# Selective scan on one core: VectorE's products half a group earlier, and ScalarE adding the carried state to 30 of 32 scans

## The chip, the core and the metric

The kernel runs on one core of one Trainium2 chip. A core has TensorE (PE, with its weight loads PEld), VectorE (DVE), ScalarE (ACT), GpSimd (POOL) and SyncE (SP, which only issues DMAs here). Each engine takes its instructions in the order in which the program lists them and waits on semaphores for the others. The metric is the device time of the whole program in microseconds.

## The reference, cut to what matters

The program is a chain of four layers on an image of shape (2, 128, 64, 64). The first three (attention, a deformable convolution block, a residual convolution block) are not touched. The fourth normalises every pixel over its channels, runs a selective scan ("mamba") over the 4096 pixels in four orders (by rows, by columns, and both reversed), and fuses the four results:

```python
def _mamba(x, W_in, conv_w, conv_b, W_xp, W_dt, b_dt, A_log, Dp, W_out):
    ...
    dt = jax.nn.softplus(dt @ W_dt.T + b_dt)
    A = -jnp.exp(A_log)
    dA = jnp.exp(dt[..., None] * A)                        # 256 channels x 16 states
    dBu = dt[..., None] * Bm[:, :, None, :] * xh[..., None]
    def step(h, inp):
        dA_t, dBu_t = inp
        h = dA_t * h + dBu_t
        return (h, h)
    ...
    y = jnp.einsum('lbdn,bln->bld', hs, Cm)
    y = y + xh * Dp
    y = y * jax.nn.silu(z)
    return y @ W_out.T
```

So for each of 256 x 16 = 4096 pairs of channel and state a first-order recurrence runs along 4096 pixels, for two images and four orders.

## The kernel before, in words

**Blocks, groups, scans.** `layer3` cuts each of the 2 x 4 sequences into 8 blocks of 512 pixels (`BLK`): 64 blocks, numbered `i`. A block has 8 groups, one for each half of the channels (`hf`) and each quarter of the states (`ng`); `k` numbers the 512 groups and `slot = k % 8` is a group's place in its block. A group has 4 scans `q` of 128 partitions x 512 pixels, so a block has 32 scans. In this document "scan 2.1" is scan `q = 1` of the group at slot 2.

**What one group needs.** PE copies the row of B to 128 partitions into a bank of PSUM (`pb`, L1692). The product B x (dt x u) for all four scans goes into an SBUF tile `db`: the first `ND[hf][ng]` columns by DVE (`db_dve`, L1713), the rest by POOL (`db_pool`, L1722). Before, DVE does five whole groups of a block and 176 of the 512 columns of slot 2; POOL does slots 1 and 6 whole and 336 columns of slot 2. ACT computes `da = exp(dt*A)` for each scan into one of three PSUM buffers (`expo`, L1735), two scans ahead of DVE (`AHEAD = 2`). DVE runs the recurrence in place (`scan`, L1749). ACT keeps the last column of the four scans (`keep`, L1754, into `hl`), POOL multiplies the group by C (`cmul`, L1759, in place, after `keep` has read it), and PE sums it over the states (`sums`, L1767).

**The carried state.** A scan of a block that isn't the first of its sequence starts from the state that the last block left. Either DVE reads it as the scan's initial value (operand `hl` in the profile's rows, "hl form" below), or ACT adds it to the first column of `db` ahead of time (L1741, 128x1) and the scan starts from zero; the kernel calls such a scan carried. Before, 20 of 32 scans are carried: all of slots 1 and 6, whose products POOL makes two groups ahead, and scans 2 and 3 of the others. L1741 directly follows the `expo` of its scan.

**The order.** Everything is issued in the order of one hand-written loop over `k` (`tc.manual_schedule`). Inside, a loop over `q` issues `expo` of the scan two ahead and then `scan(k, q)`. After the four scans come `db_dve(k + 1)`, `cmul(k - 1)`, `db_pool(k + 2)` and the work for the next block, a part for each slot. Its ACT part (`front_act`) is: slot 0 two copies of the x-projection; slot 1 a softplus of four activations (L1652 to L1655); slot 2 another, and a copy; slot 3 two copies; slot 4 a Silu of z between two table loads; slot 7 a Silu of u between two table loads. Its PE part (`front_pe`) makes what these read. `finish`, one ACT copy of 128x512, stands in slot 6 before the last `expo`. The DMAs of a group (`transfers`) stand ahead of its loop over `q`.

**Two kinds of blocks with more work.** In blocks 0 to 4 and 22 to 29 a further 512 pixels are normalised alongside ("LN blocks", 13 of 64; `next_norm`). The two matmuls of that, mean at slot 0 and variance at slot 2 (L1517, L1534), write to the same three PSUM buffers as `da`; the logarithm (`ln_log`, L1538) stands before `expo` in `q == 3` of slot 2, the store (`ln_store`, L1553) at the end of slot 6. In blocks 1 to 4 and 33 to 36 ("turn blocks") ACT also copies two pieces of the image into the other order at the end of slot 6 (`turn`, L1559).

Of the kernel before, what the change touches and what calls it, by code (L numbers as in the profile page):

```python
# [15 lines left out]
AF = mybir.ActivationFunctionType  # L16
# [8 lines left out]
BLK = 512  # L25
NBLK = L // BLK
# [1394 lines left out]
def layer3(g, I, out):  # L1421
# [5 lines left out]
    nc, tc = g.nc, g.tc  # L1427
    NJ = 4

    ND = ((BLK, 0, 176, BLK), (BLK, BLK, 0, BLK))  # L1430
    NNG = N_STATE // NJ
    HB = 1
    HC = 3
    with ExitStack() as ctx:
# [139 lines left out]
        NBK = len(blocks)  # L1574
# [134 lines left out]
        def db_dve(k):  # L1709
            i, hf, ng = groups[k]  # L1710
            n = ND[hf][ng]
            if n:
                nc.vector.tensor_tensor(  # L1713
                    db_tile(k)[:, :, :n], G[k].pop("pb")[:, :n].unsqueeze(1).to_broadcast([P, 4, n]),
                    S[i]["d4", hf][:, 1, :, :n], ALU.mult,
                )
# [9 lines left out]

        def carried(k, q):

            i, hf, ng = groups[k]
            return i % NBLK > 0 and (q >= 2 or ND[hf][ng] == 0)  # L1730

        def expo(k, q):
            i, hf, ng = groups[k]
            da = psd.tile([P, BLK], F32, name="da")
            nc.scalar.activation(da, S[i]["d4", hf][:, 0, q, :], AF.Exp, scale=am[:, hf, q, ng : ng + 1])  # L1735
            G[k]["da", q] = da
            if carried(k, q):

                first = BLK - 1 if reverse(i) else 0
                b0 = G[k]["db"][:, q, first : first + 1]  # L1740
                nc.scalar.activation(b0, da[:, first : first + 1], AF.Identity, bias=b0, scale=hl[:, hf, ng, q, :])  # L1741

        def scan(k, q):
            i, hf, ng = groups[k]
# [6 lines left out]
        def keep(k):  # L1751
            i, hf, ng = groups[k]
            last = 0 if reverse(i) else BLK - 1
            nc.scalar.copy(hl[:, hf, ng], G[k]["db"][:, :, last : last + 1])  # L1754
# [6 lines left out]
        def sums(k):  # L1761
            i, hf, ng = groups[k]
            if ng == 0:
                py = S[i]["y", hf] = psy.tile([P, BLK], F32, name="py")
                nc.tensor.matmul(py, ddp[:, hf, :], S[i]["u"][:, hf, :], start=True, stop=False)
            for q in range(4):
                nc.tensor.matmul(  # L1767
                    S[i]["y", hf][32 * q : 32 * q + 32, :], fold, G[k]["db"][:, q, :],
                    start=False, stop=(ng == NNG - 1),
                )  # L1770
            del G[k]

        def gate(i, hf):
            s_ = S[i]
            gt = s_["gt", hf] = ck.tile([P, BLK], F32, name="gt")
            nc.vector.tensor_tensor(gt, s_.pop(("y", hf)), s_["z"][:, hf, :], ALU.mult)  # L1776
# [11 lines left out]
        def finish(i):  # L1788
            b, nd, c = blocks[i]
            s_ = S.pop(i)  # L1790
            if nd == 0:
                nc.scalar.activation(s_["xv"], img(s_["pf"]), AF.Identity, bias=vec(g, "b_fuse"))  # L1792
            elif nd < 3:
                nc.scalar.copy(s_["xv"], img(s_["pf"]))
            else:
                res = ck.tile([P, BLK], F32, name="res", bufs=1)
                nc.scalar.copy(res, s_["pf"])
                nc.sync.dma_start(out[b, :, c * BLK : (c + 1) * BLK], res)

        groups = [(i, hf, ng) for i in range(NBK) for hf in range(2) for ng in range(NNG)]  # L1800
        G = {}
# [75 lines left out]
        with tc.manual_schedule():  # L1877
            tc.keep_in_program_order(nc.scalar.preload_act_table_set("natural_log_exp_and_others"))
            nc.scalar.activation(am, am, AF.Exp)
            nc.vector.tensor_scalar(am, am, -1.0, None, ALU.mult)  # L1880
            nc.vector.memset(xt[:, :HC], 0.0)
            nc.vector.memset(xt[:, HC + L :], 0.0)
            nc.vector.memset(xn[:, HB - 1, HW - HC :], 0.0)
            nc.vector.memset(xn[:, HB + HW, :HC], 0.0)
            units = [(k, q) for k in range(len(groups)) for q in range(4)]
            AHEAD = 2

            for k in range(NFIRST):
                ln_mean(0, k)
            for k in range(NFIRST):  # L1890
                ln_less(0, k)
            ln_square(0, 0)
            ln_var(0, 0)
            ln_square(0, 1)
            ln_log(0, 0)
            ln_root(0, 0)
            ln_scale(0, 0)
            ln_var(0, 1)
            ln_square(0, 2)
            ln_store(0, 0)  # L1900
            ln_var(0, 2)
            begin(0)
            conv(0, 1)
            for part in (ln_log, ln_root, ln_scale):
                for k in (1, 2):
                    part(0, k)
            conv_silu(0)
            front_pe(0, 0)
            ln_store(0, 1)
            front_act(0, 0)  # L1910
            bc_store(0)
            front_pe(0, 1)
            front_act(0, 1)
            ln_store(0, 2)
            sum_parts(0, 0)
            sum_copy(0, 0)
            spread(0, 0)
            spread_store(0, 0)
            spread_load(0, 0)
            softplus(0, 1)  # L1920
            front_pe(0, 3)
            front_act(0, 3)
            spread(0, 1)
            spread_store(0, 1)
            for ng in range(NNG):
                copies(0, "b", ng)
                copies(0, "c", ng)
            for k in range(2):
                weights(k)
            db_dve(0)  # L1930
            db_pool(0)
            front_pe(0, 4)
            front_act(0, 4)
            front_pe(0, 5)
            front_pe(0, 6)
            for u in range(AHEAD):
                expo(*units[u])
            front_act(0, 7)
            db_pool(1)
            for k in range(len(groups) + 7):  # L1940
                i, slot = divmod(k, 8)
                live = k < len(groups)
                more = k + 1 < len(groups)
                ended = 1 <= k <= len(groups)
                transfers(i + 1, slot)
                if k + 2 < len(groups):
                    weights(k + 2)
                norm = next_norm(i)
                for q in range(4):
                    if slot == 6 and q == 3 and 1 <= i <= NBK:  # L1950
                        finish(i - 1)
                    if norm and slot == 2 and q == 3:
                        ln_log(*norm)
                    if q == 0 and ended:
                        keep(k - 1)
                    if 4 * k + q + AHEAD < len(units):
                        expo(*units[4 * k + q + AHEAD])
                    if norm and q == 0:
                        if slot == 0:
                            ln_mean(*norm)  # L1960
                        elif slot == 2:
                            ln_var(*norm)
                    if live:
                        scan(k, q)

                    for j, hf in (((k - 6) // 8, 0), ((k - 10) // 8, 1)):
                        if q == 1 and 8 * j + 6 + 4 * hf == k and 0 <= j < NBK:
                            gate(j, hf)
                if norm and slot == 0:
                    ln_less(*norm)  # L1970
                if more:
                    db_dve(k + 1)
                if ended:
                    cmul(k - 1)
                if k + 2 < len(groups):
                    db_pool(k + 2)

                if slot == 5 and 0 <= k - 2 < len(groups):
                    sums(k - 2)
                if slot == 5 and 1 <= i <= NBK:  # L1980
                    project(i - 1)
                front_pe(i + 1, slot)
                front_act(i + 1, slot)
                front_pool(i + 1, slot)
                if norm:
                    if slot == 1:
                        ln_square(*norm)
                    elif slot == 3:
                        ln_root(*norm)
                    elif slot == 5:  # L1990
                        ln_scale(*norm)
                    elif slot == 6:
                        ln_store(*norm)
                if live:

                    if slot == 6 and 0 < i % (4 * NBLK) <= NBLK // 2:
                        for n in range(2):
                            turn(blocks[i][0], 2 * (i % (4 * NBLK) - 1) + n)

                if slot != 5 and 0 <= k - 2 < len(groups):  # L2000
                    sums(k - 2)
# [155 lines left out]
```

## Time and profile before

| | us |
|---|---|
| median of 3 runs | 5483.52 (5479.7 to 5484.56) |
| the profiled execution | 5481.25 |
| its span in the profile | 5479.5 |

| engine | busy, share of the span | busy in 4000 to 4500 us of the span |
|---|---|---|
| PE | 4690.7 us, 86% | 403.89 of 500 us |
| DVE | 4537.5 us, 83% | 490.28 |
| ACT | 4062.2 us, 74% | 426.38 |
| POOL | 3646.3 us, 67% | 494.15 |

The first three layers end at about 2190 us; the scan of the 64 blocks takes the other 3.3 ms. Shares over the whole span mix the layers, so the last column, a stretch inside the scan, is the one to read. An instruction's record on DVE can overlap the next one's by some tens of ns, so the distance from start to start is what an instruction costs a full queue, not the length of its record.

### The profile page before, as it was taken

Reading aid. Unit: us, or ns where it says so; the run is one execution under the profiler, and the core shown is the slowest. Engines: PE = TensorE matmul, PEld = TensorE weight load, DVE = VectorE, ACT = ScalarE, POOL = GpSimd, SP = SyncE. Lnnn points to the kernel's source line nnn. Section 1 sums busy time; section 2 is a strip of 40 time slices with the busy share of each in tenths; the row PEclk is TensorE's granted clock in tenths of the full one; section 3 lists DMA queues with packets and bytes.
Section 4 is the critical chain, followed back from the end, with each engine's and each line's share of the span. In section 5 each row is a group of like instructions: output and inputs, shape, how many; then the busy total and the mean of one; then the engine's idle time right before and its main releaser. Section 6 shows DMA issues by size and latency. Waiting matters only on the chain.

```text
span 5479.5 us, 54616 instructions
## 1 busy us (share of the span) xinstructions
PE 4690.7 (86%) x17062; PEld 1753.3 (32%) x17062; DVE 4537.5 (83%) x4280; ACT 4062.2 (74%) x6242; POOL 3646.3 (67%) x1205
## 2 busy tenths in 40 slices
PE   7999999999996998778777887878888777888776
PEld 3444444344453443222222222222222222222221
DVE  7666655661356995999999999999999999999998
ACT  4999999500365114898888888888898888888886
POOL 5232222200001111999999999999999999999998
PEclk9999999999998999888888788888778888788887
DMA  4111110300672001555556556555555556556554
GB/s 171 43 42 33 39 31 24 66 7 16 113 138 54 0 0 44 139 126 143 135 125 148 131 128 143 127 138 143 135 134 141 134 128 146 134 126 148 135 131 103
DMA packets 331017, 554.08 MB, mean 101 GB/s; under 512 B 53456, under 2 KB 112736, under 8 KB 330720
## 3 DMA queue, kind: packets, MB, share of 16 engines
q1 hardware_dynamic: 329568, 549.86, 42.2%
q8 instruction: 135, 2.21, 0.2%
q14 instruction: 162, 1.33, 0.1%
q10 hardware_dynamic: 1152, 0.68, 0.1%
HBM read 461.20 MB, written 89.13 MB: 100 GB/s over the span
## 4 chain that ended last, share of the span: by engine, by line
DVE 45%; PE 36%; ACT 10%; issue 5%; DMA 2%; POOL 1%; SPq 0%; DVEq 0%; POOLq 0%; ACTq 0%
DVE db L1749 30%; DVE db L1713 11%; PE ps L424 8%; PE acc L440 8%; PE m L1311 6%; PE m L715 5%; ACT da L1735 4%; PE acd L1027 2%; ACT db L1741 1%; DVE gt L1776 1%; PE m L675 1%; ACT L1600 1%; ACT u L1600 1%; PE pf L990 1%; PE pm L1619 1%
## 5 line engine op out<-in xcount | busy, mean ns | idle before, releaser
L1759 POOL TENSOR_TENSOR db<-db,c 128x2048 f32<-128x2048 f32 x512 | 2312.8, 4532 | 45.6 <-ACT hl L1754 30.6
L1735 ACT ACTIVATE da<-dd,am 128x512 f32<-128x512 f32 x2048 | 1398.4, 687 | 298.8 <-DVE db L1749 279.8
L1749 DVE TENSOR_TENSOR_SCAN db<-da,db 128x512 f32<-128x512 f32 x1376 | 1584.4, 1202 | 34.6 <-ACT db L1741 26.9
L430 ACT ACTIVATE e<-ps 128x1536 f16<-128x1536 f32 (+1 forms) x683 | 919.7, 1631 | 23.5 <-PE ps L424 23.5
L1749 DVE TENSOR_TENSOR_SCAN db<-da,hl,db 128x512 f32<-128x512 f32 x672 | 825.7, 1270 | 40.6 <-POOL db L1722 2.3
L1713 DVE TENSOR_TENSOR db<-pbc,dd 128x2048 f32<-128x2048 f32 (+1 forms) x384 | 780.1, 2031 | 31.3 <-DMA dd<-dx 31.3
L1722 POOL TENSOR_TENSOR db<-b,dd 128x2048 f32<-128x2048 f32 (+1 forms) x192 | 772.9, 4026 | 12.7 <-DMA b<-bx 12.7
L1767 PE MATMUL py<-db,fold 128*32 128x512 f32 x4096 | 602.6, 674 | 151.2 <-POOL db L1759 151.1
L424 PE MATMUL ps<-q 128*128 128x512 f16 x2048 | 553.5, 379 | 3.2 <-issue 2.0
L440 PE MATMUL acc<-e,v 128*128 128x512 f16 x2048 | 553.2, 379 | 0.1
L352 POOL TENSOR_TENSOR parts<-parts 32x512 f32<-32x512 f32 x63 | 79.2, 1257 | 655.0 <-DVE parts L351 655.0
L1741 ACT ACTIVATE db<-da,db,hl 128x1 f32<-128x1 f32 x1120 | 393.7, 352 | 146.1 <-DVE db L1713 103.4
L1362 POOL MEMSET v<- 128x256 f32 x2 | 1.1, 550 | 623.7 <-DVE b L1210 623.7
L1311 PE MATMUL m<-v,u 128*128 128x512 f32 x864 | 377.3, 600 | 34.4 <-DVE v L1261 32.6
L346 DVE RECIPROCAL rec<-acc 32x512 f32<-32x512 f32 x63 | 211.6, 3359 | 201.3 <-PE acc L440 201.0
L1660 PE MATMUL pm<-dd,ident 128*128 128x512 f32 x512 | 359.8, 841 | 2.7 <-ACT dd L1653 2.7
L1619 PE MATMUL pm<-u,wxp 128*72 128x512 f32 x256 | 180.6, 846 | 139.7 <-ACT u L1600 139.7
L1692 PE MATMUL pbc<-bc,sel 64*128 64x512 f32 x384 | 206.7, 538 | 102.6 <-DVE db L1713 102.0
L424 PEld LDWEIGHTS <-q 128*128 128x128 f16 x2048 | 197.5, 97 | 273.1 <-issue 92.0
L440 PEld LDWEIGHTS <-v 128*128 128x128 bf16 x2048 | 199.2, 97 | 248.1 <-issue 9.3
L1767 PEld LDWEIGHTS py<-db,fold 128*32 128x32 f32 x4096 | 90.6, 114 | 552.3 <-issue 328.1
L1595 PE MATMUL pm<-xn,wcs 128*128 128x512 f32 x512 | 234.4, 601 | 17.4 <-ACT xa L1792 6.4
(361 smaller groups left out, 6572.8 us busy)
## 6 DMA issues: line engine op xcount, KB each, us to landing
dd<-dx SPq DMA_DIRECT2D x1024, 256.0 KB, 6.5
dx<-dd SPq DMA_DIRECT2D x128, 512.0 KB, 5.5
c<-bx SPq DMA_DIRECT2D x1024, 64.0 KB, 2.1
b<-bx SPq DMA_DIRECT2D x512, 64.0 KB, 4.6
early<-pos SPq DMA_DIRECT2D x104, 256.0 KB, 10.1
piece<-qd SPq DMA_DIRECT2D x128, 128.0 KB, 2.7
piece<-kd SPq DMA_DIRECT2D x112, 128.0 KB, 2.7
hats<-pos SPq DMA_DIRECT2D x32, 256.0 KB, 10.5
```

What stands on the lines that cost most here:

```text
L424: nc.tensor.matmul(ps[:, i, :], t[:, 1, kb * P : (kb + 1) * P], t[:, 0, qb * BLK : (qb + 1) * BLK], start=True, stop=True,)
L430: nc.scalar.activation(e[:, :n, :], ps[:, :n, :], AF.Exp, scale=1.0 / UP**2)
L440: nc.tensor.matmul(acc, v3[b][:, kb, h, :], e[:, i, :], start=(kb == 0), stop=(kb == NS - 1))
L1311: nc.tensor.matmul(m[x], weights[j][:, dy, x, :], v[j][b][:, x, r0 : r0 + RP, :].rearrange("p r i -> p (r i)"), start=(dy == 0), stop=(dy ...
L1660: nc.tensor.matmul(ps, g.ident, S[i]["dd", hf][:, x, :], start=(x == 0), stop=(x == 1))
L1713: nc.vector.tensor_tensor(db_tile(k)[:, :, :n], G[k].pop("pb")[:, :n].unsqueeze(1).to_broadcast([P, 4, n]), S[i]["d4", hf][:, 1, :, :n], A ...
L1722: nc.gpsimd.tensor_tensor(db_tile(k)[:, :, n:], S[i]["b", ng][:, n:].unsqueeze(1).to_broadcast([P, 4, BLK - n]), S[i]["d4", hf][:, 1, :, n ...
L1735: nc.scalar.activation(da, S[i]["d4", hf][:, 0, q, :], AF.Exp, scale=am[:, hf, q, ng : ng + 1])
L1741: nc.scalar.activation(b0, da[:, first : first + 1], AF.Identity, bias=b0, scale=hl[:, hf, ng, q, :])
L1749: nc.vector.tensor_tensor_scan(d1, d0, d1, 0.0 if zero else hl[:, hf, ng, q, :], ALU.mult, ALU.add)
L1759: nc.gpsimd.tensor_mul(v, v, S[i]["c", ng].unsqueeze(1).to_broadcast([P, 4, BLK]))
L1767: nc.tensor.matmul(S[i]["y", hf][32 * q : 32 * q + 32, :], fold, G[k]["db"][:, q, :], start=False, stop=(ng == NNG - 1),)
```

## The change

`db_dve(k + 1)` moves from the end of group `k` to the middle, behind scan 1, and `front_pe` and `front_act` move from the end of the group to behind scans 1 and 2. L1741 becomes a function of its own, `carry`, and all scans of a block that has a predecessor are carried but 0.0 and 5.0. For scan 0 of a group the carry is issued one step later than its `expo`, that is, behind `front_act`. DVE takes 240 columns of slot 2 in place of 176. `finish` moves from the fourth step of slot 6 to the first. The `transfers` of a group stay where they are.

```diff
-    ND = ((BLK, 0, 176, BLK), (BLK, BLK, 0, BLK))
+    ND = ((BLK, 0, 240, BLK), (BLK, BLK, 0, BLK))
...
         def carried(k, q):
-            i, hf, ng = groups[k]
-            return i % NBLK > 0 and (q >= 2 or ND[hf][ng] == 0)
+            return groups[k][0] % NBLK > 0 and not (q == 0 and k % 8 in (0, 5))
...
             nc.scalar.activation(da, S[i]["d4", hf][:, 0, q, :], AF.Exp, scale=am[:, hf, q, ng : ng + 1])
             G[k]["da", q] = da
+
+        def carry(k, q):
+            i, hf, ng = groups[k]
             if carried(k, q):
                 first = BLK - 1 if reverse(i) else 0
                 b0 = G[k]["db"][:, q, first : first + 1]
-                nc.scalar.activation(b0, da[:, first : first + 1], AF.Identity, bias=b0, scale=hl[:, hf, ng, q, :])
+                a0 = G[k]["da", q][:, first : first + 1]
+                nc.scalar.activation(b0, a0, AF.Identity, bias=b0, scale=hl[:, hf, ng, q, :])
...
                 for q in range(4):
-                    if slot == 6 and q == 3 and 1 <= i <= NBK:
-                        finish(i - 1)
                     if norm and slot == 2 and q == 3:
                         ln_log(*norm)
                     if q == 0 and ended:
                         keep(k - 1)
+                    if q == 3 and more:
+                        carry(k + 1, 0)
                     if 4 * k + q + AHEAD < len(units):
-                        expo(*units[4 * k + q + AHEAD])
+                        n = units[4 * k + q + AHEAD]
+                        expo(*n)
+                        if q != 2:
+                            carry(*n)
+                    if slot == 6 and q == 0 and 1 <= i <= NBK:
+                        finish(i - 1)
...
+                    if q == 1:
+                        if more:
+                            db_dve(k + 1)
+                        if slot == 5 and 0 <= k - 2 < len(groups):
+                            sums(k - 2)
+                        if slot == 5 and 1 <= i <= NBK:
+                            project(i - 1)
+                        front_pe(i + 1, slot)
+                    if q == 2:
+                        front_act(i + 1, slot)
                 if norm and slot == 0:
                     ln_less(*norm)
-                if more:
-                    db_dve(k + 1)
                 if ended:
                     cmul(k - 1)
                 if k + 2 < len(groups):
                     db_pool(k + 2)
-                if slot == 5 and 0 <= k - 2 < len(groups):
-                    sums(k - 2)
-                if slot == 5 and 1 <= i <= NBK:
-                    project(i - 1)
-                front_pe(i + 1, slot)
-                front_act(i + 1, slot)
                 front_pool(i + 1, slot)
```

## The prediction

> **What bounds the kernel now.** I read the busy time by stretches first. In the scan neither DVE nor POOL has 2% to spare, and ACT is at 85%:
>
> ```profile
> 4000.00:4500.00 500.00, 403.89 (x1196) 125.32 (x1194) 490.28 (x393) 426.38 (x784) 494.15 (x129) 0.84 0.57 135
> ```
>
> (length; busy PE, PEld, DVE, ACT, POOL.) Then the groups:
>
> ```profile
> L1735 ACT ACTIVATE da<-dd,am 128x512 f32<-128x512 f32 x2048 | 1398.4, 687 | 298.8 <-DVE db L1749 279.8
> L1749 DVE TENSOR_TENSOR_SCAN db<-da,db 128x512 f32<-128x512 f32 x1376 | 1584.4, 1202 | 34.6 <-ACT db L1741 26.9
> L1749 DVE TENSOR_TENSOR_SCAN db<-da,hl,db 128x512 f32<-128x512 f32 x672 | 825.7, 1270 | 40.6 <-POOL db L1722 2.3
> L1741 ACT ACTIVATE db<-da,db,hl 128x1 f32<-128x1 f32 x1120 | 393.7, 352 | 146.1 <-DVE db L1713 103.4
> ```
>
> DVE idles mainly for L1741; ACT idles for DVE, as `expo` needs a PSUM buffer that a scan frees. The chain of waits over 3000 to 5400 us gives 70% to L1749 and L1713, 9% to L1735 and L1741, hardly any to POOL. So DVE and ACT set the pace, POOL follows closely. The timeline of DVE gives the price of each step from start to start:
>
> ```profile
> 4036.01 2.27 DVE L1713 TENSOR_TENSOR db<-pbc,dd 128x2048 f32<-128x2048 f32 x1
> 4038.38 2.46 DVE L1749 TENSOR_TENSOR_SCAN db<-da,hl,db 128x512 f32<-128x512 f32 x2
> 4040.79 4.57 DVE L1749 TENSOR_TENSOR_SCAN db<-da,db 128x512 f32<-128x512 f32 x4
> 4045.76 2.34 DVE L1749 TENSOR_TENSOR_SCAN db<-da,db 128x512 f32<-128x512 f32 x2 [0.40 <-ACT db L1741]
> 4048.01 0.87 DVE L1713 TENSOR_TENSOR db<-pbc,dd 128x704 f32<-128x704 f32 x1
> ...
> 4051.39 0.67 DVE L1776 TENSOR_TENSOR gt<-py,z 128x512 f32<-128x512 f32 x1
> 4051.97 2.33 DVE L1749 TENSOR_TENSOR_SCAN db<-da,db 128x512 f32<-128x512 f32 x2
> ```
>
> A carried scan is 1.115 us ((4.57 - 1.20)/3 and its like), the hl form 1.19 (2.37 for two in most blocks), a product followed by a scan that reads it 2.37. The gate, followed by a scan that doesn't read it, is 0.58 for a record of 0.67. A block: 20 x 1.115 + 12 x 1.19 + 5 x 2.37 + 1.00 (176 columns) + 2 x 0.58 = 50.6. The last block, with no front work beside it, takes just that (5396.95 to 5447.54). Plain blocks take 51.17 (4019.37 to 4070.54): DVE waits about 0.5 for ACT at scan 1.2. ACT there:
>
> ```profile
> 4035.01 0.69 ACT L1735 ACTIVATE da<-dd,am 128x512 f32<-128x512 f32 x1 [0.42 <-DVE db L1749]
> 4035.72 1.28 ACT L1600 ACT_TABLE_LOAD   x1
> 4037.01 1.26 ACT L1600 ACTIVATE u<-pm,vecs 128x512 f32<-128x512 f32 x2
> 4038.29 1.28 ACT L1601 ACT_TABLE_LOAD   x1
> 4039.59 0.20 ACT L1754 COPY hl<-db 128x4 f32<-128x4 f32 x1
> 4039.69 0.69 ACT L1735 ACTIVATE da<-dd,am 128x512 f32<-128x512 f32 x1
> 4040.41 0.35 ACT L1741 ACTIVATE db<-da,db,hl 128x1 f32<-128x1 f32 x1
> 4040.66 0.68 ACT L1735 ACTIVATE da<-dd,am 128x512 f32<-128x512 f32 x1
> ```
>
> From here ACT stands still nowhere until 4053. `expo` with carry is 0.97 (0.72 + 0.25), `expo` alone 0.61, `keep` 0.10, the Silu of u 3.87.
>
> **The change part by part. DVE gains.** Ten scans a block leave the hl form: 10 x 0.075 = 0.75. The products are no longer followed by a scan that reads them: no row shows that pair. Its ends are 2.37 as now and 2.27 - 0.09 = 2.18 as the gate overlaps; I take 2.18, the gate being the same operation with the same PSUM source: 6 x 0.19 = 1.1. The 64 columns of slot 2 cost 256 x 1.04 ns = 0.27 ((2265 - 865) ns over 1344 elements). An hl scan behind a plain one isn't shown either; 1.19, twice a block, between 1.115 and 1.30. A block of DVE: 48.94.
>
> **POOL gains** 256 x 2.12 ns = 0.54 (4524 and 3029 ns). It was busy 50.42 of the 51.17 (idle 0.25 and 0.50 for `keep`), so its floor is 49.9.
>
> **ACT pays** 10 more carries a block, and its front work now stands ahead of the carry of the next group's scan 0: whatever delays it delays that carry, and DVE behind it. I lay the two queues side by side from T, the end of scan 7.1, which frees the buffer of `expo` for scan 0.0. ACT, in its new order:
> - start and `expo` for 0.0: 0.84 (0.13 after the scan, then 0.71 to the load above); Silu of u with its loads: 3.87
> - `expo` and carry for 0.1: 0.97; `keep` of slot 7, then 0.2 and 0.3: 2.04
> - `expo` for 1.0: 0.61; the two copies: 0.95 (4043.62 to 4044.57); carry of 1.0: 0.25
> - 1.1: 0.97; `keep`, 1.2 and 1.3: 2.04; `expo` for 2.0: 0.61; softplus: 2.43 (4047.82 to 4050.25); carry of 2.0 and on to DVE: 0.38
>
> That is 15.96. DVE in the same time: product of slot 0 2.18, scans 7.2 and 7.3 2.23, slot 0 4.54, slot 1 4.46 (no product behind it), product of slot 2 1.05: it wants scan 2.0 at 14.46. So DVE stalls 1.5 a block: 0.2 at 0.1, 0.5 at 1.0, 0.8 at 2.0. Counted in this way the old order gives 0.47 where the row above shows 0.40. In the other slots a product of 2.18 between scans 1 and 2 covers the front work: 3.0 has 0.45 to spare, 5.1 nothing (Silu of z, 3.68, is covered just so), 6.0 has 0.36.
> Plain block: 48.94 + 1.5 = 50.44, or -0.73; 41 of them, **-30**. Six plain blocks at the head of a sequence, without carries, go from 49.85 to 48.8: **-6**.
>
> **LN blocks lose.** There the variance takes a `da` buffer, so the `expo` of 3.0 waits for scan 2.2 (first row; L1538 is the logarithm, L1652 begins the softplus of slot 2):
>
> ```profile
> 3590.36 0.69 ACT L1735 ACTIVATE da<-dd,am 128x512 f32<-128x512 f32 x1 [0.32 <-DVE db L1749]
> 3590.99 0.67 ACT L1538 ACTIVATE sq<-da,cst 128x512 f32<-128x512 f32 x1
> 3591.56 0.68 ACT L1735 ACTIVATE da<-dd,am 128x512 f32<-128x512 f32 x1
> 3592.17 0.67 ACT L1652 ACTIVATE dd<-pm,vecs 128x512 f32<-128x512 f32 x1
> ```
>
> The program of the changed kernel keeps that wait, and softplus, copy, logarithm and carry of 3.0 now follow it: 0.13 + 0.61 + 2.9 + 0.57 + 0.38 = 4.6, while DVE has one scan left, 1.1 (its product is ahead of 2.2 now). Stall 3.5. At slot 0 the mean's matmul holds the x-projection until 6.0 to 6.9 us after scan 0.0 starts; the carry of 1.0 now stands behind its copies: ready at 7.8 on average, wanted at 5.1, stall 2.65 up to there. Block: 48.94 + 0.58 (L1527) + 2.65 + 0.8 + 3.5 = 56.5, against 52.56 now (3292.67 to 3713.12, eight blocks): +3.9, seven times, **+27**. Turn blocks: 2.1 us of copies now stand three scans ahead of the Silu of u: 1.8 late, net +1.1, four times, **+4**. Four that are both: 3.3 + 0.8 + 3.5 of stalls, +4.4, **+18**. Two LN blocks at the head of a sequence have no carries, but `expo` waits behind the same work: **+4**.
>
> **Costed at nothing.** The moved PE work: the x-projection ends at T + 6.2, read at T + 8.3; the projection for `finish` about 0.6 before it, and the product and gate of slot 6 (2.8) cover more. POOL's product of slot 1 ends 4.1 after slot 7 (4040.03), carry 1.0 comes 4.9 after; beyond these 0.8 us it would cost one for one. SP: `transfers` stay; what they wait for (L1625, L1663) comes half a group earlier, `finish`'s 16 stores too; the loads of `dd` landed 15 us ahead of slot 4's product. The first three layers are the same.
>
> **Two rules.** The rows have 1.29 from a table load to the next instruction. The Trainium skill, "ScalarE: Activation LUTs", What ACT_TABLE_LOAD costs, adds a drain of about 1.38 to each load of 1.28. Two loads stand in front of 0.1 and of 5.1, neither with slack: 5.5 a block more, some +300. The row decides: no drain. The same section gives an activation 186 ns, 93 for each pointer operand, 93 overlapped: a carry would be an estimated 0.28. The rows charge 0.97 - 0.61 = 0.36. With 0.28 the eight carries on the path above take 0.64 off the stall; that is the first rival.
>
> **Sum.** -30 - 6 + 27 + 4 + 18 + 4 = +17 on the profiled execution's 5481.25; the median is 2.3 above it: 5500.
>
> **The rivals.** *Faster: POOL becomes the bound.* If ACT is less late than counted, a plain block falls to POOL's 49.9, -1.27: 41 x -1.27 = -52, heads -6, turn +2, LN +44: 5471; with LN stalls half as long 5450. It decides at a stall of about 1.1 a plain block instead of 1.5. For it: only 0.05 per carry separates the two. Against it: my count is made of whole observed steps. *Slower still: the product keeps its 2.37.* 1.1 more on DVE, 0.4 less stall: +0.75 in 58 blocks and a little at heads: 5547. For it: the pair was never seen; against it: the gate. *The change isn't what it says:* the program's order shows the moves, and 112 hl scans left.
>
> **How the numbers follow.** About 0.2%, 11 us, is what a measurement of this kernel can tell from no change. My count, 0.55, own range 5488 to 5515; POOL as bound 0.28; the slow product 0.12; the rest something unseen. A quarter of the first and part of the second lie within 11 us: faster 0.24, same 0.2, slower 0.56. Range 5456 to 5535: it takes in most of the fast rival and stops short of the slow one.
>
> **What would show it.** DVE idle before L1751 for ACT of about 1.5 us in plain blocks, at 0.1, 1.0, 2.0; in LN blocks over 6 us, the longest at 3.0; plain blocks of 50.4 from start to start, LN blocks of 56; products at 2.18; POOL idle growing. Wrong: plain blocks at 49.9 with POOL without a gap, LN blocks under 54, or products at 2.37.

## The result, and the profile after

| | before | after |
|---|---|---|
| median of 6 runs each, us | 5482.53 (5479.28 to 5484.56) | 5515.10 (5512.32 to 5519.91) |
| profiled execution, us | 5481.25 | 5517.35 |
| its span, us | 5479.5 | 5515.6 |

The ratio is 1.0061, with a 95% interval of 1.0048 to 1.0074: the change costs 33 us. Forecast were 5500, with a range of 5456 to 5535, and "slower" as the likeliest of the three.

The same stretch of 500 us as before (no LN blocks, a few turn blocks at its start; length; busy PE, PEld, DVE, ACT, POOL; granted clock, share of the DMA engines, GB/s):

```profile
4000.00:4500.00 500.00, 389.51 (x1187) 118.18 (x1186) 484.67 (x393) 451.99 (x876) 488.30 (x128) 0.86 0.59 137
```

ACT went from 426 to 452 us, DVE and POOL from 490 and 494 to 485 and 488: both now have gaps. The groups of the page after say for whom they wait (last columns: idle time just before the group, and what ended most of it):

```profile
L1761 POOL TENSOR_TENSOR db<-db,c 128x2048 f32<-128x2048 f32 x512 | 2313.1, 4535 | 113.0 <-ACT hl L1756 110.2
L1751 DVE TENSOR_TENSOR_SCAN db<-da,db 128x512 f32<-128x512 f32 x1936 | 2222.7, 1202 | 146.3 <-ACT db L1743 131.3
L1734 ACT ACTIVATE da<-dd,am 128x512 f32<-128x512 f32 x2048 | 1406.5, 688 | 205.0 <-DVE db L1751 197.9
L1743 ACT ACTIVATE db<-da,db,hl 128x1 f32<-128x1 f32 x1680 | 589.2, 351 | 147.6 <-DVE db L1713 90.7
```

Before, DVE's waits for the carry (L1741) came to 27 us; for the same line, now L1743, they are 131. ACT's own waits for a `da` buffer fell from 280 to 198, and POOL's L1761 now stands 110 us for `keep` (L1756; 31 us before), which waits in ACT's queue as well. Neither the table of engines nor "the busiest engine" shows this: DVE is busy 37 us less than before, and the program takes 36 longer. The page's chain of waits gives 12% to DMAs, 2% before; but in the table of waits from 2200 us on, DMAs account for 0.4 us in all, so they are not the cause.

One plain block on DVE, from the product of slot 0 on:

```profile
4488.79 2.26 DVE L1713 TENSOR_TENSOR db<-pbc,dd 128x2048 f32<-128x2048 f32 x1
4490.97 2.32 DVE L1751 TENSOR_TENSOR_SCAN db<-da,db 128x512 f32<-128x512 f32 x2
4493.22 1.25 DVE L1751 TENSOR_TENSOR_SCAN db<-da,hl,db 128x512 f32<-128x512 f32 x1
4494.59 3.45 DVE L1751 TENSOR_TENSOR_SCAN db<-da,db 128x512 f32<-128x512 f32 x3
4498.43 2.34 DVE L1751 TENSOR_TENSOR_SCAN db<-da,db 128x512 f32<-128x512 f32 x2 [0.38 <-ACT db L1743]
4500.68 1.13 DVE L1713 TENSOR_TENSOR db<-pbc,dd 128x960 f32<-128x960 f32 x1
4501.73 2.33 DVE L1751 TENSOR_TENSOR_SCAN db<-da,db 128x512 f32<-128x512 f32 x2
4504.69 2.34 DVE L1751 TENSOR_TENSOR_SCAN db<-da,db 128x512 f32<-128x512 f32 x2 [0.64 <-ACT db L1743]
...
4525.29 1.25 DVE L1751 TENSOR_TENSOR_SCAN db<-da,hl,db 128x512 f32<-128x512 f32 x1
4526.54 4.57 DVE L1751 TENSOR_TENSOR_SCAN db<-da,db 128x512 f32<-128x512 f32 x4
```

In order these are: product of slot 0; scans 7.2, 7.3; scan 0.0 in the hl form; 0.1 to 0.3; 1.0 and 1.1 after a stall; the partial product of slot 2; 1.2, 1.3; 2.0 and 2.1 after a second stall; and, half a block later, 5.0, the other hl scan. A full product and the scan after it, which no longer reads it, are 2.18 apart. From 4488.79, where the product follows scan 7.1, to the start of scan 2.0 at 4504.69 it is 15.90 us.

ACT in the first half of that time:

```profile
4488.90 0.69 ACT L1734 ACTIVATE da<-dd,am 128x512 f32<-128x512 f32 x1
4489.61 1.28 ACT L1600 ACT_TABLE_LOAD   x1
4490.91 1.26 ACT L1600 ACTIVATE u<-pm,vecs 128x512 f32<-128x512 f32 x2
4492.19 1.28 ACT L1601 ACT_TABLE_LOAD   x1
4493.48 0.69 ACT L1734 ACTIVATE da<-dd,am 128x512 f32<-128x512 f32 x1
4494.21 0.35 ACT L1743 ACTIVATE db<-da,db,hl 128x1 f32<-128x1 f32 x1
```

The first row is the `expo` of scan 0.0, 0.11 after scan 7.1 gave its buffer free; the last is the carry of 0.1. No idle entry stands in any row of ACT from here until the carry of 2.0 at 4504.33, after which scan 2.0 starts 0.36 later. So in this stretch ACT is the pace and DVE waits for it. A wait as short as that of 0.1 gets no idle entry; it shows in the starts, 1.37 us from 0.0 to 0.1.

For a table by kind of block I take the distance between the starts of the partial product of slot 2 in one block and in the next (an interval so holds the end of one block and the start of the other), in the timelines of all 64 blocks. The 12 intervals at a head so hold about as much of a plain block as of a head:

| intervals | before | after | sum of the difference |
|---|---|---|---|
| plain, 33 | 51.20 | 50.62 | -19.1 |
| at the head of a sequence, 12 | 50.50 | 49.99 | -6.2 |
| turn alone, 4 | 51.17 | 52.36 | +4.8 |
| with LN blocks, 14 | 52.28 | 56.17 | +54.4 |

That is 33.9 of the 36.1 us; the rest lies ahead of the first and behind the last of these intervals.

An LN block on DVE (scans 0.1 to 0.3; the subtraction of L1527; 1.0 and 1.1; then, after the left-out rows, 2.2 and 2.3; 3.0 and 3.1):

```profile
3553.78 3.59 DVE L1751 TENSOR_TENSOR_SCAN db<-da,db 128x512 f32<-128x512 f32 x3 [0.89 <-ACT db L1743]
3557.29 0.66 DVE L1527 TENSOR_TENSOR xc<-xa,da 128x512 f32<-128x512 f32 x1
3559.81 2.34 DVE L1751 TENSOR_TENSOR_SCAN db<-da,db 128x512 f32<-128x512 f32 x2 [1.86 <-ACT db L1743]
...
3571.11 2.33 DVE L1751 TENSOR_TENSOR_SCAN db<-da,db 128x512 f32<-128x512 f32 x2
3576.85 2.34 DVE L1751 TENSOR_TENSOR_SCAN db<-da,db 128x512 f32<-128x512 f32 x2 [3.41 <-ACT db L1743]
```

and ACT beside the last of these stalls:

```profile
3572.36 0.69 ACT L1734 ACTIVATE da<-dd,am 128x512 f32<-128x512 f32 x1 [2.80 <-DVE db L1751]
3572.99 0.67 ACT L1652 ACTIVATE dd<-pm,vecs 128x512 f32<-128x512 f32 x1
3573.56 0.68 ACT L1653 ACTIVATE dd<-pm,vecs 128x512 f32<-128x512 f32 x1
3574.13 0.63 ACT L1654 ACTIVATE dd<-dd 128x512 f32<-128x512 f32 x1
3574.79 0.72 ACT L1655 ACTIVATE dd<-dd,cst 128x512 f32<-128x512 f32 x1
3575.42 0.57 ACT L1663 COPY dd<-pm 128x512 f32<-128x512 f32 x1
3575.88 0.69 ACT L1538 ACTIVATE sq<-da,cst 128x512 f32<-128x512 f32 x1
3576.46 0.35 ACT L1743 ACTIVATE db<-da,db,hl 128x1 f32<-128x1 f32 x1
```

ACT itself idles 2.80 us for scan 2.2, since the variance holds a `da` buffer; then the front work of slot 2 and the logarithm run, and only then the carry that scan 3.0 waits for.

### The profile page after: what moved, and what is told of

It is laid out like the page before. It is cut to its first block, busy times and chain, and to the rows that moved or that the text cites. A ratio compares the mean times of both kernels' runs of the same rounds, so it can differ in the third digit from the quotient of the medians.

```text
span 5515.6 us, 54866 instructions
## 1 busy us (share of the span) xinstructions
PE 4615.6 (84%) x17062; PEld 1712.8 (31%) x17062; DVE 4500.9 (82%) x4280; ACT 4204.0 (76%) x6802; POOL 3613.4 (66%) x1205
## 4 chain that ended last, share of the span: by engine, by line
PE 34%; DVE 29%; ACT 16%; DMA 12%; issue 5%; POOL 3%; SPq 2%; POOLq 0%; DVEq 0%; ACTq 0%
DVE db L1751 18%; PE ps L424 8%; PE acc L440 8%; DVE db L1713 8%; PE m L1311 6%; ACT da L1734 5%; DMA dd<-dx 5%; PE m L715 5%; DMA c<-bx 4%; ACT db L1743 2%; POOL db L1761 2%; PE acd L1027 2%; PE m L675 1%; ACT dd L1655 1%; DMA early<-pos 1%
## 5 line engine op out<-in xcount | busy, mean ns | idle before, releaser
L1761 POOL TENSOR_TENSOR db<-db,c 128x2048 f32<-128x2048 f32 x512 | 2313.1, 4535 | 113.0 <-ACT hl L1756 110.2
L1751 DVE TENSOR_TENSOR_SCAN db<-da,db 128x512 f32<-128x512 f32 x1936 | 2222.7, 1202 | 146.3 <-ACT db L1743 131.3
L1769 PE MATMUL py<-db,fold 128*32 128x512 f32 x4096 | 644.2, 715 | 404.0 <-POOL db L1761 403.4
L1713 DVE TENSOR_TENSOR db<-pbc,dd 128x2048 f32<-128x2048 f32 (+1 forms) x384 | 798.7, 2080 | 31.3 <-DMA dd<-dx 31.3
L1722 POOL TENSOR_TENSOR db<-b,dd 128x2048 f32<-128x2048 f32 (+1 forms) x192 | 740.4, 3857 | 13.9 <-DMA b<-bx 13.9
L1743 ACT ACTIVATE db<-da,db,hl 128x1 f32<-128x1 f32 x1680 | 589.2, 351 | 147.6 <-DVE db L1713 90.7
L1660 PE MATMUL pm<-dd,ident 128*128 128x512 f32 x512 | 332.9, 784 | 3.5 <-ACT dd L1653 3.0
L1311 PEld LDWEIGHTS m<-v,u 128*128 128x128 f32 x864 | 165.6, 192 | 246.2 <-issue 229.7
L1595 PE MATMUL pm<-xt,wcs 128*128 128x512 f32 x512 | 233.6, 598 | 0.0
L1619 PE MATMUL pm<-u,wxp 128*72 128x512 f32 x256 | 156.4, 744 | 92.2 <-ACT u L1600 92.2
```

What stands on the lines that cost most here:

```text
L1311: nc.tensor.matmul(m[x], weights[j][:, dy, x, :], v[j][b][:, x, r0 : r0 + RP, :].rearrange("p r i -> p (r i)"), start=(dy == 0), stop=(dy ...
L1595: nc.tensor.matmul(pu, wcs[:, hf, s, :], window(blk, sgn * s), start=(s == 0), stop=(s == 3))
L1713: nc.vector.tensor_tensor(db_tile(k)[:, :, :n], G[k].pop("pb")[:, :n].unsqueeze(1).to_broadcast([P, 4, n]), S[i]["d4", hf][:, 1, :, :n], A ...
L1722: nc.gpsimd.tensor_tensor(db_tile(k)[:, :, n:], S[i]["b", ng][:, n:].unsqueeze(1).to_broadcast([P, 4, BLK - n]), S[i]["d4", hf][:, 1, :, n ...
L1743: nc.scalar.activation(b0, a0, AF.Identity, bias=b0, scale=hl[:, hf, ng, q, :])
L1751: nc.vector.tensor_tensor_scan(d1, d0, d1, 0.0 if zero else hl[:, hf, ng, q, :], ALU.mult, ALU.add)
```

## The experiments

The open question after the result was which part of the change costs the time. Two theories: (A) the place of the front work, ahead of the carries, makes the stalls, and moving it out of the way in the slots where it stalls brings the time back; (B) the ten added carries make ACT late, and the place of the rest matters little. The expectations also name (C), that POOL or the earlier products set the pace. The runs are told by subject, not in the order of time. Ratios are against the kernel before, timed beside each kernel on the same chip.

### The front work of slot 2 at the end of the group, in LN blocks only

```diff
-                    if q == 2:
+                    if q == 2 and not (norm and slot == 2):
                         front_act(i + 1, slot)
...
+                if norm and slot == 2:
+                    front_act(i + 1, slot)
```

> The changed kernel, but in the 13 LN blocks the front work of slot 2 stays at the end of the group, behind the carry of 3.0 and the step of 3.1. Theory A (the order of waits in few blocks: front work stands behind an expo that waits for scan 2.2): the stall of 3.4 us at 3.0 falls to about 0.5 at 3.2, so about 2.9 in 11 blocks and 2.2 in two, -36: about 5479. Theory B (ACT has too much to do: 560 more carries of 0.35): no work is taken away, so 5515 within 5. Theory C (POOL or the earlier products set the pace): 5515.

Measured: 5502.87, ratio 1.0042 (1.0025 to 1.0059). Only a third of what A expects came back. The stall of 3.4 did go, but DVE in an LN block then shows (stalls at 3.0, 3.2, 4.0 and 5.1):

```profile
3562.74 2.34 DVE L1751 TENSOR_TENSOR_SCAN db<-da,db 128x512 f32<-128x512 f32 x2 [0.49 <-ACT db L1743]
3565.00 2.27 DVE L1713 TENSOR_TENSOR db<-pbc,dd 128x2048 f32<-128x2048 f32 x1
3567.68 2.34 DVE L1751 TENSOR_TENSOR_SCAN db<-da,db 128x512 f32<-128x512 f32 x2 [0.42 <-ACT db L1743]
3570.73 2.34 DVE L1751 TENSOR_TENSOR_SCAN db<-da,db 128x512 f32<-128x512 f32 x2 [0.71 <-ACT db L1743]
...
3579.68 5.68 DVE L1751 TENSOR_TENSOR_SCAN db<-da,db 128x512 f32<-128x512 f32 x5 [1.01 <-ACT db L1743]
```

That is 2.6 us in four pieces in place of 3.4 at 3.0 and 0.2 at 5.1. ACT's work was put off, not taken away, and what comes after it is late in its turn.

### The front work of slots 0 and 1 at the end of the group, in all blocks

The edit is the same with `slot in (0, 1)` as its condition.

> The changed kernel, but the front work of slots 0 and 1 stays at the end of the group in all blocks, so that the partial product of slot 2 and the gate with the product of slot 3 lie behind it. Theory A: the stalls at 1.0 (0.38) and 2.0 (0.7) go, a plain block falls from 50.65 to POOL's floor of about 49.9; in LN blocks 1.9 at 1.0 and 0.65 at 2.0 go too, about 0.3 comes back at 1.2: about -30 in plain, -25 in LN and turn blocks, 5460. Theory B: same work, 5515. Theory C: if the early products were at fault, 5515 too.

Measured: 5516.44, ratio 1.0065 (1.0048 to 1.0082): no gain at all. The stall of 1.0 is gone; those of 2.0 and 3.0 took its place (first two rows, DVE; the third is ACT's carry of 2.0):

```profile
4492.27 2.34 DVE L1751 TENSOR_TENSOR_SCAN db<-da,db 128x512 f32<-128x512 f32 x2 [0.44 <-ACT db L1743]
...
4501.46 2.34 DVE L1751 TENSOR_TENSOR_SCAN db<-da,db 128x512 f32<-128x512 f32 x2 [1.83 <-ACT db L1743]
4491.89 0.35 ACT L1743 ACTIVATE db<-da,db,hl 128x1 f32<-128x1 f32 x1 [1.48 <-POOL db L1722]
```

The plain intervals rose from 50.62 to 51.22 (+20 us over 33), those with LN blocks fell from 56.17 to 54.78 (-19 over 14). The plain ones are of two kinds, and the third row says why. This block belongs to a reversed sequence, whose scans begin at column 511, in POOL's part of slot 2. With the front work out of its way ACT comes to the carry of 2.0 before POOL has written that column, and its whole queue stands for 1.48 us. The 17 plain intervals of reversed sequences rose from 50.57 to 51.93. In the 16 of the others the carry reads column 0, which DVE writes; there ACT does not wait, what is left of the stall shows at 3.0, and they fell from 50.68 to 50.47, not to the 49.9 that A expects. A in its simple form has fallen: the place of ACT's work mostly decides where the stall shows.

### The old rule of 20 carries, everything else as changed

```diff
-            return groups[k][0] % NBLK > 0 and not (q == 0 and k % 8 in (0, 5))
+            i, hf, ng = groups[k]
+            return i % NBLK > 0 and (q >= 2 or ND[hf][ng] == 0)
```

> The changed kernel with the old rule for carries (20 of 32 scans, the others in the hl form); all that was moved stays moved. Theory A: DVE pays 0.75 a block, the path of ACT between 7.1 and 2.0 is 0.7 shorter, 3.0 in LN blocks waits 0.8 less: plain block about 50.3, in all about -25: 5490. Theory B: 197 us of ACT work gone, the loss against before goes and the gain of the earlier products shows: 5450 or less. Theory C: 0.75 a block more on DVE, 5550.

Measured: 5461.26, ratio 0.9964 (0.9950 to 0.9978): faster than before, and 54 us faster than after; A expected 5490, B 5450 or less. Plain intervals are 49.94 in most places, with one stall of 0.20 left and no idle entry on POOL, close to the 49.9 that the prediction gave as POOL's floor; LN ones are 54.62. So the rest of the change (early products, moved front work, `finish`, 64 columns) gains 20 us together, and the ten carries lose more than twice that. What each part of the rest is worth was not run.

### The product with 176 columns on DVE

`ND` of slot 2 goes from 240 back to 176; nothing else.

> The changed kernel with 176 columns of slot 2 on DVE as before. Theory A: the product of slot 2 is 0.27 shorter, so the stall at 2.0, which is behind ACT's work, is 0.27 longer; POOL's floor of 50.4 is still under 50.65: same time, 5515 within 4. Theory C (POOL is the bound): +0.54 in 64 blocks, 5550. DVE alone as bound: -17.

Measured: 5515.72, ratio 1.0065 (1.0048 to 1.0081), the same as with 240. DVE has 0.27 us less to do in a block; its idle before 2.0 grew by just that (0.64 to 0.91, and 0.70 to 0.97 in the other blocks), and the plain block stayed at 50.61 to 50.68. This is how a block looks whose length another engine sets; C is out for plain blocks. There POOL does 0.54 more without harm. Not so in the six plain blocks at the head of a sequence, which have no carries: from scan 0.0 to the next 0.0 they take 49.33 in the changed kernel and 49.86 here, 0.53 more, with no idle entry on POOL in either. They are POOL's.

### Which carries: the three on the path, or the other seven

B can mean two things: each carry costs its 0.36 us wherever it stands (load), or only where ACT is the one waited for (place). Two complementary kernels tell these apart. The first drops the added carries of 0.1, 2.0 and 2.1, on the path or right behind it, and keeps seven; the second keeps these three and drops the seven:

```diff
 # 27 carries
-            return groups[k][0] % NBLK > 0 and not (q == 0 and k % 8 in (0, 5))
+            return groups[k][0] % NBLK > 0 and (k % 8, q) not in ((0, 0), (0, 1), (2, 0), (2, 1), (5, 0))
 # 23 carries
-            return groups[k][0] % NBLK > 0 and not (q == 0 and k % 8 in (0, 5))
+            return groups[k][0] % NBLK > 0 and (q >= 2 or k % 8 in (1, 6) or (k % 8, q) in ((0, 1), (2, 0), (2, 1)))
```

> The changed kernel with three of its ten added carries taken out: those of scans 0.1, 2.0 and 2.1, which stand on the path from scan 7.1 to scan 2.0. Theory 'place' (a carry costs where ACT is the one waited for): three carries of 0.36 us leave the path, DVE pays 3 x 0.075 us for three hl forms; the stall of a plain block falls from 1.05 us to 0.2 or less, a plain block takes 50.0, the whole about 5480. Theory 'load' (each of the ten added carries costs alike, wherever it stands): three tenths of the 54 us that all ten cost, about 5499.

> The converse: of the ten added carries those of 0.1, 2.0 and 2.1 stay, and the other seven (3.0, 3.1, 4.0, 4.1, 5.1, 7.0, 7.1) are taken out. Theory 'place': the stall of the plain block stays at about 1 us and DVE pays 7 x 0.075 us more, so a plain block takes about 51.1 and the whole 5530 to 5543. Theory 'load': seven tenths of 54 us come back, 5477.

Measured: 27 carries, 5475.09, ratio 0.9980 (0.9972 to 0.9988); 23 carries, 5520.27, ratio 1.0061 (1.0044 to 1.0078), the ratio of the full change. Taking three carries out brings 0.8% of the time, taking seven out brings nothing. Load is refuted: it wanted the opposite order. Between 4000 and 4500 us ACT is busy 452 us with 27 carries, as with 30, and 434 with 23: the slower of the two kernels is the one in which ACT has less to do.

The block with 27 carries (0.0 and 0.1 in the hl form; 0.2, 0.3; 1.0, 1.1; product; 1.2, 1.3; 2.0 and 2.1 in the hl form):

```profile
4512.53 2.44 DVE L1751 TENSOR_TENSOR_SCAN db<-da,hl,db 128x512 f32<-128x512 f32 x2
4514.88 2.32 DVE L1751 TENSOR_TENSOR_SCAN db<-da,db 128x512 f32<-128x512 f32 x2
4517.40 2.34 DVE L1751 TENSOR_TENSOR_SCAN db<-da,db 128x512 f32<-128x512 f32 x2 [0.20 <-ACT db L1743]
4519.65 1.13 DVE L1713 TENSOR_TENSOR db<-pbc,dd 128x960 f32<-128x960 f32 x1
4520.70 2.33 DVE L1751 TENSOR_TENSOR_SCAN db<-da,db 128x512 f32<-128x512 f32 x2
4523.12 2.46 DVE L1751 TENSOR_TENSOR_SCAN db<-da,hl,db 128x512 f32<-128x512 f32 x2
```

From the end of 7.1 (4508.11 in the same timeline) to 2.0 it is 15.0 us, 0.9 less than with 30 carries, although three scans have the dearer form. Here ACT has made `expo` of 2.0 (first row) ahead of the softplus (its last step in the second row):

```profile
4520.25 0.68 ACT L1734 ACTIVATE da<-dd,am 128x512 f32<-128x512 f32 x1
4522.67 0.72 ACT L1655 ACTIVATE dd<-dd,cst 128x512 f32<-128x512 f32 x1
```

So the carry of 2.0 was worth more than its own 0.36. It stands behind the softplus; without it scan 2.0 needs `expo` alone and starts at 4523.12, before the softplus has ended. With 30 carries scan 2.0 started 0.99 after that last step did, which here would be 4523.66: an estimated 0.54 of the 0.9, the other 0.36 being the carry of 0.1. Neither was dropped alone. The block with 23 carries keeps both stalls (1.0 and 2.0):

```profile
4491.19 3.45 DVE L1751 TENSOR_TENSOR_SCAN db<-da,db 128x512 f32<-128x512 f32 x3
4495.03 2.34 DVE L1751 TENSOR_TENSOR_SCAN db<-da,db 128x512 f32<-128x512 f32 x2 [0.39 <-ACT db L1743]
...
4501.31 2.34 DVE L1751 TENSOR_TENSOR_SCAN db<-da,db 128x512 f32<-128x512 f32 x2 [0.65 <-ACT db L1743]
```

Here 7.1 ends at 4485.36, so the path is 15.95: that of the full change, with seven carries fewer on ACT. Its plain intervals are 50.97, near the 51.1 expected. That the whole isn't slower than after, where "place" expected 5530 to 5543, is due to the LN blocks: 55.36 against 56.17, since the carries of 3.0 and 3.1 that they lose do stand on the LN blocks' own path. I had left that out.

### All front work at the end of the group, with the early product and 30 carries

The edit is that of the first experiment without a condition.

> The changed kernel with ScalarE's front work back at the end of the group, in all slots; the early product and the 30 carries stay. By the count with da buffers: the expo of scan 0.1 waits for scan 7.2, which now has the product in front of it, so the Silu of u ends 8.2 us after scan 7.1 and scan 0.2 is wanted at 6.6: stalls of 2.5 to 3.7 us at 0.2, the like at 5.2 (Silu of z), about 1 at 2.2: plain blocks of 55 to 57 us, the whole 5730 to 5880. If the place of the front work did not matter, 5515.

Measured: 5703.36, ratio 1.0398 (1.0381 to 1.0415). Plain intervals are 54.74; the stalls are at 5.2 and 0.2, behind the two Silus, at two of the three places expected; the 1 us expected at 2.2 did not come, and the sum is somewhat below the bottom of the range of the count. At 5.2 (the first row is scan 5.0, in the hl form):

```profile
4525.15 1.27 DVE L1751 TENSOR_TENSOR_SCAN db<-da,hl,db 128x512 f32<-128x512 f32 x1
4526.32 1.21 DVE L1751 TENSOR_TENSOR_SCAN db<-da,db 128x512 f32<-128x512 f32 x1
4530.21 4.57 DVE L1751 TENSOR_TENSOR_SCAN db<-da,db 128x512 f32<-128x512 f32 x4 [2.68 <-ACT db L1743]
```

Before, the product lay between the front work and the scan that needed ACT next, and covered it. Moved two scans ahead, it covers another stretch, and the front work has to move with it. The two moves are one change, shown here with 30 carries; the carries are another.

### The copies of `turn` earlier

```diff
+                    if q == 1 and live and slot == 6 and 0 < i % (4 * NBLK) <= NBLK // 2 and early(i):
+                        for n in range(2):
+                            turn(blocks[i][0], 2 * (i % (4 * NBLK) - 1) + n)
...
-                    if slot == 6 and 0 < i % (4 * NBLK) <= NBLK // 2:
+                    if slot == 6 and 0 < i % (4 * NBLK) <= NBLK // 2 and not early(i):
```

`early(i)` is `i % (4 * NBLK) < 4 or i >= 4 * NBLK`: all turn blocks but block 4, whose copies read what the last `ln_store` writes.

> The changed kernel with turn alone moved: in eight turn blocks its two copies stand in the second quarter of slot 6 instead of its end. By the prediction's step (the copies make the Silu of u, and with it the carry of 0.1, about 1.8 us late) the stall of 1.8 at 0.1 goes, so turn blocks fall from 52.4 to 50.7: 4 x 1.7 for turn-only and up to 4 x 2.3 for those that are both: about 5500 to 5504. If ACT passes it on to 6.x or 1.0, no change: 5515.

Measured: 5506.48, ratio 1.0046 (1.0031 to 1.0061). The turn-only intervals fell from 52.36 to 50.68, those of plain blocks, so the stall of 1.8 at 0.1 was the copies' doing. In the blocks that are both there was hardly a gain (56.90 to 56.83 over the four intervals with their copies): in blocks 2 and 3 the 2.3 us at 0.1 became 0.5 at 0.1 and 2.1 to 2.3 at 1.0.

### A kernel from these parts

Four combinations, all with turn early: the 20 carries with slot 2's front work late in LN blocks; the 27 and the 20 with slots 0 and 2 late in LN blocks; and the last with 27 carries in plain blocks and 20 in LN blocks, whose rule is

```diff
+            i, hf, ng = groups[k]
+            if next_norm(i):
+                return i % NBLK > 0 and (q >= 2 or ND[hf][ng] == 0)
+            return i % NBLK > 0 and (k % 8, q) not in ((0, 0), (0, 1), (2, 0), (2, 1), (5, 0))
...
+                    if q == 2 and not (norm and slot in (0, 2)):
                         front_act(i + 1, slot)
...
+                if norm and slot in (0, 2):
+                    front_act(i + 1, slot)
```

> The kernel of the 20 carries (5461), with two things more: in the LN blocks ScalarE's front work of slot 2 stands at the end of the group, and the copies of turn stand in the second quarter of slot 6 in the four turn blocks after the first sequences and the blocks of the last layer half. With 20 carries ACT has room, so the stall of 2.6 us at 3.1 in thirteen LN blocks goes for the most part, -20, and turn gives 8 x 1 us: about 5435. If ACT only passes its lateness on, as in the run with 30 carries, -6 to -10: about 5453.

> The kernel of the 27 carries (0.998 of before) with ScalarE's front work of slots 0 and 2 at the end of the group in the LN blocks, and the copies of turn in the second quarter of slot 6 in eight turn blocks. The LN blocks lose the 3.4 us stall at 3.0 (or a part of it, passed on to 3.1 and 4.0) and the 1.3 to 2.2 us at 1.0: from 55 to 56 down to about 52.5, 13 x 3 us = -39; turn -8 x 1.5 = -12: about 5425, ratio 0.989. If the LN blocks pass the lateness on as with 30 carries (12 us of 36 gained there), about 5450.

> The same with 20 carries: against the run with 20 carries that had slot 2 alone moved (0.9934), the 2.6 us at 1.0 goes in about ten LN blocks: -20, ratio about 0.990. Plain blocks stay at 49.96, 0.2 above those with 27 carries, so this should end about equal to the 27: within 10 us either way. If the stall at 1.0 isn't due to the place of the copies, no change: 0.9934.

> The two last kernels combined: 27 carries in the plain blocks (49.83 there) and 20 in the LN blocks (53.6 there), front work of slots 0 and 2 at the end of the group in LN blocks, turn early in eight blocks. Theory 'place': the LN blocks' remaining stalls of 0.4 to 1.0 us between slots 3 and 5 are those of carries that stand in late ACT work and go with the carries; plain blocks keep their 0.1 to 0.2 gain: 10 LN blocks x 0.5 and 40 x 0.12, so 5 to 8 below the better of the two: about 5433 (ratio 0.9915). Theory 'load': between the two or equal, 5439 to 5443.

| kernel | median, us | ratio to before (95%) | plain | LN |
|---|---|---|---|---|
| 20 carries, slot 2 late in LN | 5449.46 | 0.9934 (0.9918 to 0.9951) | 50.07 | 53.65 |
| 27 carries, slots 0 and 2 late in LN | 5442.59 | 0.9931 (0.9917 to 0.9944) | 49.86 | 53.91 |
| 20 carries, the same | 5439.04 | 0.9926 (0.9913 to 0.9940) | 50.06 | 53.26 |
| 27 plain, 20 in LN blocks | 5433.58 | 0.9913 (0.9900 to 0.9927) | 49.89 | 53.25 |

The first three fell short of what was expected of them, the last did not. In the first the stall at 1.0 was still there, mostly 1.8 to 2.7; with slot 0 late it fell to about 0.9 in most LN blocks (third row), which is where LN blocks went from 53.65 to 53.26. In the second the LN blocks passed their lateness on, with stalls of mostly 0.4 to 1.0 from slot 3 to slot 5, as in the first experiment; with 20 carries 0.3 at 3.2 and 0.6 at 5.1 are left of these. The intervals of the ratios overlap, so the order of these four rests on the block columns: the last kernel has the plain block of the one parent and the LN block of the other, as "place" expected. It beats the kernel before by 0.87%, about 47 us, and the changed one by 1.5%. What bounds it outside LN blocks can be read in the window row:

```profile
4000.00:4500.00 500.00, 390.81 (x1215) 120.38 (x1211) 496.46 (x402) 454.32 (x871) 500.00 (x132) 0.86 0.59 138
```

POOL is busy all of the 500 us. ACT has as much to do as in the changed kernel (454 us and 452) and costs nothing. In its LN blocks, too, the longest single stall is mostly POOL's, in front of scan 2.0, though ACT's (0.9 at 1.0, 0.3 at 3.2, 0.6 at 5.1) are more in sum (L1754 is the scan in this kernel):

```profile
3522.50 2.46 DVE L1754 TENSOR_TENSOR_SCAN db<-da,hl,db 128x512 f32<-128x512 f32 x2 [0.94 <-POOL db L1722]
```

Whether columns moved from POOL to DVE would now pay was not tried.

## Why the prediction was right, point by point

**The mechanism was right.** The path from scan 7.1 to scan 2.0 was counted at 15.96 us and takes 15.90, with stalls where the prediction put them: 0.20 at 0.1 (forecast 0.2), 0.46 at 1.0 (0.5), 0.72 at 2.0 (0.8), taken as starts against the same steps without a stall. The two kernels with 27 and 23 carries show that it is this path, and not ACT's load, that sets the plain block. The product without a reader is 2.18 to 2.20, as taken from the gate, so the rival of 2.37 is out.

**DVE's gain was taken too high.** The plain block shown takes 50.61 us. Without the stalls of the path and one of 0.08 at 5.1 it is 49.14, not 48.94. The thirty plain scans make nearly all of this: they take 1.121 each (33.64 in all, from start to start), not 1.115, as the scan behind a product or a stall takes 1.13 or 1.14. As ACT sets the stretch from 7.1 to 2.0, only what lies outside it reached the block: 34.70 there against 50.44 - 15.96 = 34.48. The 0.08 is part of it. The prediction had 5.1 "covered just so", but it waits for its carry:

```profile
4526.16 0.35 ACT L1743 ACTIVATE db<-da,db,hl 128x1 f32<-128x1 f32 x1
```

The carry ends at 4526.51 and scan 5.1 starts at 4526.54, 1.25 after 5.0, where an hl scan costs 1.17 (last section). A plain interval gained 0.58 instead of 0.73.

**The terms, like for like.** From each scan 0.0 to the next, as the prediction counts its blocks, and in the profiled executions:

| blocks | forecast | measured |
|---|---|---|
| plain and turn, 45 (44 measured) | -26 | -14.9 |
| plain at the head of a sequence, 6 | -6 | -3.1 |
| LN, 7 | +27 | +30.3 |
| LN and turn, 4 | +18 | +18.2 |
| LN at the head of a sequence, 2 | +4 | +4.3 |
| ahead of the first 0.0 and behind the last | 0 | +1.3 |
| sum | +17 | +36.1 |

The direction and most parts were right. Of the missing 19 us, 11 are in plain blocks, most of it the 0.17 to 0.24 by which these are longer than 50.44.

**Heads.** They go from 49.85 to 49.33, not to 48.8. The forecast was that of DVE alone and lay below the 49.9 that the prediction itself gives as POOL's floor. POOL has no idle entry there, DVE waits 0.29 for its product at 2.0, and the run with 176 columns moved these blocks by 0.53 for POOL's 0.54.

**LN blocks.** The idle entries of the block shown are 0.89, 1.86, 0.64, 3.41 and 0.18, 6.98 in all; the prediction had 2.65 + 0.8 + 3.5 = 6.95. The longest stands at 3.0 and its cause is the row it was read from. An idle entry leaves out the 0.08 by which the records of two scans overlap where nothing is waited for; from start to start the stalls are 7.5, and the block takes 57.25 for the forecast 56.5. The mean of the seven is 57.00.

**Turn.** The stall at 0.1 is 1.8 as counted, and the four intervals show +4.8 for +4.

**The rival of the faster side** had POOL as the bound with plain blocks at 49.9. It was not wrong in what it saw: take out the carries of 0.1, 2.0 and 2.1, and plain blocks are at 49.85 on average, with no idle entry on POOL. (By the prediction's own sums it decides at a stall of 49.9 - 48.94 = 0.96, not at 1.1.) But in the changed kernel a carry on ACT costs 0.97 - 0.61 = 0.36 as its rows said (4494.55 to 4495.52 with, in the last kernel's ACT timeline 3530.10 to 3530.71 without), not the 0.28 estimated from the Trainium skill ("ScalarE: Activation LUTs", What ACT_TABLE_LOAD costs). Nor do the rows of after show the drain that the same section adds to a table load: `expo` ends 0.02 before the load at 4489.61, and from there to the next instruction it is 1.30 us, with a load of 1.28. In both places the row of the trace was the one to take.

**What the prediction did not ask** is which part of the change to keep. It priced ten carries at a gain of 0.75 for DVE and a stall of 1.5, and did not price the version that leaves three of them out, though two of them (0.1 and 2.0) stand in its own list of the path, the second right behind the softplus.

## What to carry to other kernels

When work is moved from a full engine to one with slack, ask at each place whether the receiver is being waited for there; with 452 of 500 us busy in both, 27 carries were harmless and 30 cost 44 us more (0.81% of 5482), by three instructions of 0.36 us in each block, one of which made a scan wait for a softplus. Lay the two queues side by side from one known release to the next wait, and place what is moved only outside the stretch in which the receiver has no idle entry. Moving the receiver's other work about within such a stretch mostly moved the stall here (0.2 us of a plain block gained at best). And each instruction that is moved brings its own waits into the receiver's queue: reached early, one carry stopped all of ACT for 1.48 us.

## What was not expected of the hardware

A scan that starts from a state in memory (hl form) costs 0.06 us more than one that starts from zero, whether it stands alone or in a pair. Alone, with no wait behind it, it is 1.17 from start to start (4525.15 to 4526.32 in the kernel with all front work at the end; the same in all 112 such scans of that run), against 1.115. Two in a row take 2.35 in the kernel with 27 carries (4512.53 to 4514.88), against 2.23. The 1.25 of scan 5.0 in the changed kernel looks like a dearer scan, but holds the wait for the carry of 5.1. No idle entry tells of it; the two records touch, where they overlap by 0.08 without a wait.
